# Inverse square roots of head norms in an fp8 attention block: from VectorE instructions to GpSimd instructions

## The chip, the core and the metric

The kernel runs on one NeuronCore of a Trainium2 chip. The metric is the device time of one execution, in microseconds (us); lower is better. Each core has a matrix engine (TensorE, "PE" in the profile, with its weight loads as "PEld"), VectorE ("DVE"), ScalarE ("ACT"), GpSimd ("POOL") and SyncE ("SP"), each with its own instruction queue, worked in order. Engines wait for each other by semaphores.

## What is computed

The program is a decoder of twelve blocks on an activation of 4 batches x 256 tokens x 256 features. The change touches the eleventh block only, an attention with fp8-rounded inputs, of 16 query heads in 4 groups, each head of 128 elements, once on its own tokens and once on a context. Its core, cut from the reference:

```
def _ln(x, w, b):
    mu = jnp.mean(x, axis=-1, keepdims=True)
    var = jnp.mean(jnp.square(x - mu), axis=-1, keepdims=True)
    return (x - mu) * jax.lax.rsqrt(var + EPS) * w + b      # EPS = 1e-05
...
q  = _ln(_fp8_linear_pertensor(ln_out, wq,  wq_scale,  q_in_scale).reshape(b, s, g, hpg, d), qln_w, qln_b)
k  = _ln(_fp8_linear_pertensor(ln_out, wk,  wk_scale,  k_in_scale).reshape(b, s, g, d),      kln_w, kln_b)
v  = _fp8_linear_pertensor(ln_out, wv, wv_scale, v_in_scale).reshape(b, s, g, d)
core = _gqa(q, k, v)
qx = _ln(..., qxln_w, qxln_b);  kx = _ln(..., kxln_w, kxln_b)      # vx likewise, from cond
xout = _gqa(qx, kx, vx)
catq = _div_clamp_fp8(concatenate([core, xout], -1), proj_smooth)
return catq @ wproj.T * (proj_in_scale * proj_w_scale)
```

Every head vector of q, qx, k and kx is thus divided by the square root of its own variance plus 1e-5. The means are already taken out of the weights, so that the variance is the sum of squares over 128.

## The kernel before, in words

The block is `l3_xattn` (line 1558). Its work is cut into 16 passes (`class Pass`, line 1664): pass n handles one of the 4 head groups and one of the 4 batches, so 4 query heads on the own tokens and the same 4 on the context, which makes 8 attention steps i = 0 to 7.

The front of pass n+1 runs during pass n. `product(t, n)` (line 1693) multiplies a tile t of 128 tokens with the weights of q, qx, or k and kx. ScalarE copies the product from PSUM into the tile `x` (128 x 12 heads x 128, line 1706), and squares it into `sq` (line 1708). VectorE sums the squares per head into `ssq` (128 x 12, line 1710). When all three products of a token tile are there, the closure `norm` (line 1712) is due: it turns the 12 sums per token into 12 factors and multiplies `x` by them. In the kernel before, VectorE makes the factors: one multiplication (L1714), `k.rsqrt` (line 108: an addition L113, a shift L117, an affine step on the bits L118, three Newton steps of three instructions each, L120 to L122), and one multiplication (L1716). GpSimd then scales `x` (L1717). Later TensorE transposes the scaled tile (`turned`, L1733).

An attention step is: `scores` (TensorE L1746), maximum (VectorE L344, tile `smx`), exponentials with their sums (ScalarE L354, tile `prob`), `divide` (VectorE's reciprocal L1753 into `sinv`, then GpSimd's multiplication of `prob` by it, L1754), `turn` (TensorE transposes `prob`, L1762, and ScalarE copies it out, L1765), `values` (TensorE L492, VectorE's scaling L1773, and for each second head the rounding to fp8, `bf16_to_e4m3fn`, L205 to L209 on VectorE). `output` (TensorE L1787, VectorE L176) projects the pass before.

The order in which all these go to the engines is written out by hand, and for this block TensorE, ScalarE, VectorE and GpSimd keep it exactly (`ORDERED`, line 2093). In step i the order is: transposes of `x` for the next pass or step (table `TURNS`), scores of i, then `flush` (line 1835: sums of squares and any norm that is due), weight preparation, parts of the next pass's products, `turn` of step i-2, `values` of step i-3, `divide` of step i. By the table `PARTS`, the product of k for token tile 0 is in step 1 and that for tile 1 in step 2, and each is flushed one step later; so the norm of tile 0 is issued in step 2 and that of tile 1 in step 3. The text calls them the first and the second norm of a pass. There are 16 x 2 = 32 norms: two before the first pass, and two in each of the first 15 passes.

In steps that the tables `THIRDS` and `OUT_THIRDS` name, GpSimd also subtracts parts of the weights (L1634, about 1 to 2 us each). In the last two passes, steps of the routing of the next block are put in between.

Of the kernel before, what the change touches and what calls it, by code (L numbers as in the profile page):

```python
# [12 lines left out]
F32 = mybir.dt.float32  # L13
# [7 lines left out]
ALU = mybir.AluOpType  # L21
AX = mybir.AxisListType

P = 128
# [1533 lines left out]
def l3_xattn(k):  # L1558
# [7 lines left out]
    nc, a, v = k.nc, k.a, k.nc.vector  # L1566
# [4 lines left out]
    ws = k.t([P, 12], F32, "ws", 1)  # L1571
# [3 lines left out]
    ws2 = k.t([P, 12], F32, "ws2", 1)  # L1575
    v.tensor_mul(ws2, ws, ws)
    v.tensor_scalar_mul(ws2, ws2, 1.0 / P)
    lnw = k.t([P, 8], F32, "lnw", 1)
    for i, n in enumerate(("q", "qx", "k", "kx")):
        f = 1.0 / math.sqrt(128.0) if i < 2 else 1.0  # L1580
# [83 lines left out]
    class Pass:  # L1664
# [28 lines left out]
        def product(self, t, n):  # L1693

            i = KINDS.index(n)
            if i == 0:
                self.x[t] = k.t([P, 12, P], F32, "x", 3)
                self.ssq[t] = k.t([P, 12], F32, "ssq", 3)
            ps = k.bank()
            if i < 2:  # L1700
                self.thrice(ps, t, n)
            else:
                self.thrice(ps[:, :256], t, "k")
                self.once(ps[:, 256:], t, "kx")
            hs = slice(4 * i, 4 * i + 4)
            nc.scalar.copy(flat(self.x[t][:, hs, :]), ps)
            sq = k.t([P, 4, P], F32, "sq", 2)
            nc.scalar.activation(flat(sq), ps, AF.Square)
            ssq, x = self.ssq[t], self.x[t]
            later.append(lambda: v.tensor_reduce(ssq[:, hs], sq, AX.X, ALU.add))  # L1710

            def norm():
                rs = k.t([P, 12], F32, "hrs", 2)
                v.tensor_tensor(rs, ssq, ws2, ALU.mult)  # L1714
                r = k.rsqrt(rs, 1e-5, "hr")
                v.tensor_tensor(rs, r, ws, ALU.mult)  # L1716
                nc.gpsimd.tensor_tensor(x, x, rs.unsqueeze(2).to_broadcast([P, 12, P]), ALU.mult)  # L1717

            if i == 2:
                later.append(norm)  # L1720
# [135 lines left out]
    for n in range(16):  # L1856
        hg, b = n // 4, n % 4
        nxt = Pass(n + 1) if n + 1 < 16 and b < 3 else None
        for i in range(8):
            g = len(line)  # L1860
# [66 lines left out]
def l3_ffn(k):  # L1927
# [157 lines left out]
BLOCKS = [  # L2085
    l0_attn, l0_xattn, l0_ffn, l1_attn, l1_xattn, l1_ffn,
    l2_attn, l2_xattn, l2_ffn, l3_attn, l3_xattn, l3_ffn,
]

# [136 lines left out]
```

## Time and profile before

| what | value |
|---|---|
| median of 3 runs | 2508.18 us (2507.96 to 2512.40) |
| the profiled execution: its own time | 2510.34 us |
| the profiled execution: its span in the trace | 2508.60 us |
| busy, whole span | PE 1935.5, DVE 1651.4, ACT 1073.0, POOL 731.4 us |
| this block's stretch, 1480 to 2260 us: busy | PE 627.7, DVE 615.1, ACT 451.7, POOL 342.4 of 780 us |
| L1717, scaling of `x` on POOL | 32 times, mean 2754 ns |
| L1754, division of `prob` on POOL | 128 times, mean 1050 ns |
| DMA issues that belong to a norm | none |

The profile is of one execution. A line of its timeline gives the start in us from the beginning of the span, the duration in us, the engine, the source line, the operation, the tiles (out<-in), shapes and a count; a bracket at its end says how long the engine stood idle just before, and what it waited for. A wait for several semaphores is put down to the one that came last by the profile. A line of the list of waits gives the waiting group, what it waited for, the total in us, how often, and the longest. A line of the table by stretches gives the stretch, its length, then busy time of PE, PEld, DVE, ACT and POOL with instruction counts, the granted TensorE clock, the DMA share and GB/s.

### The profile page before, as it was taken

What the parts mean: (1) busy time and instruction counts of PE and PEld (TensorE: products, weight loads), DVE (VectorE), ACT (ScalarE), POOL (GpSimd) and SP (SyncE); (2) the same over time, 40 slices, a digit from 0 to 9 for tenths busy, and PEclk for the clock granted to TensorE, in tenths of its full rate; (3) what the DMA queues carried; (4) which work ended last, traced back from release to release, by engine and by line L of the source; (5) the groups of instructions that cost most, each with busy time, mean ns of one, the idle gap of its engine ahead of it and who ended that gap; (6) DMA issues with size and microseconds to landing.
All of it is one profiled execution on the core that took longest, in us unless ns stands there. A gap on an engine that the chain in (4) does not pass through costs nothing. (4 is left out here: it accounts for less than half of the span.)

```text
span 2508.6 us, 32404 instructions
## 1 busy us (share of the span) xinstructions
PE 1935.5 (77%) x11369; PEld 1322.6 (53%) x11403; DVE 1651.4 (66%) x3987; ACT 1073.0 (43%) x2492; POOL 731.4 (29%) x593
## 2 busy tenths in 40 slices
PE   5999966797885789776577663778988889886784
PEld 3565553454442445543355442556766667764573
DVE  5534448545567543475798896888787777776455
ACT  1322311233345233332666643655656666552242
POOL 1311200001001000010565654335445444433452
PEclk9999987898997899986788876989999999997897
DMA  4001010601502600011012201001010000000796
GB/s 126 1 1 34 1 55 34 208 1 52 168 27 68 191 1 1 13 34 68 9 59 68 85 0 34 1 18 34 1 51 1 16 15 1 2 1 35 256 314 214
DMA packets 100868, 144.10 MB, mean 57 GB/s; under 512 B 10369, under 2 KB 80002, under 8 KB 100450
## 3 DMA queue, kind: packets, MB, share of 16 engines
q1 hardware_dynamic: 91682, 129.35, 16.0%
q0 software_dynamic: 4560, 12.59, 1.3%
q8 instruction: 90, 1.47, 0.2%
q10 hardware_dynamic: 4464, 0.09, 0.1%
q14 instruction: 72, 0.59, 0.1%
HBM read 89.26 MB, written 52.76 MB: 57 GB/s over the span
## 5 line engine op out<-in xcount | busy, mean ns | idle before, releaser
L354 ACT ACTIVATE prob<-mm,smx 128x256 f32<-128x256 f32 x392 | 184.0, 478 | 377.5 <-DVE smx L344 364.6
L548 DVE TENSOR_REDUCE mt<-pair 128x2 f32<-128x512 f32 (+1 forms) x256 | 133.4, 584 | 198.6 <-PE pair L541 198.5
L1350 PE MATMUL acc<-unit,c 128*128 128x256 f32 x512 | 153.4, 448 | 86.3 <-DVE unit L1348 53.6
L1754 POOL TENSOR_TENSOR prob<-prob,sinv 128x512 f32<-128x512 f32 x128 | 134.4, 1050 | 235.8 <-DVE sinv L1753 154.5
L1350 PEld LDWEIGHTS acc<-unit,c 128*128 128x128 f32 x512 | 108.9, 222 | 125.8 <-DVE unit L1348 68.8
L580 ACT ACTIVATE pt<-pair 128x768 f32<-128x768 f32 (+1 forms) x128 | 103.5, 861 | 153.3 <-PE pair L574 153.3
L1346 DVE TENSOR_TENSOR_SCAN h<-da,unit 128x1024 f32<-128x1024 f32 x64 | 146.8, 2293 | 31.4 <-POOL unit L1344 14.5
L1341 ACT ACTIVATE da<-dt,na 128x256 f32<-128x256 f32 x256 | 121.6, 478 | 98.0 <-DVE h L1346 92.5
L1344 POOL TENSOR_TENSOR unit<-du,bcb 128x1024 f32<-128x1024 f32 x64 | 150.0, 2367 | 31.5 <-DVE h L1346 17.7
L344 DVE TENSOR_REDUCE smx<-mm 128x2 f32<-128x512 f32 x196 | 133.2, 680 | 35.5 <-PE mm L480 21.3
L363 POOL TENSOR_TENSOR prob<-prob,sinv 128x512 f32<-128x512 f32 x68 | 71.9, 1058 | 275.9 <-DVE sinv L484 161.7
L492 PE MATMUL acc<-pt,c 128*128 128x256 f32 x512 | 136.3, 390 | 3.8 <-ACT pt L1765 3.8
L1717 POOL TENSOR_TENSOR x<-x,hrs 128x1536 f32<-128x1536 f32 x32 | 88.1, 2754 | 130.3 <-DVE hrs L1716 106.1
L181 POOL TENSOR_TENSOR c<-c,w 128x256 f32<-128x256 f32 x24 | 16.9, 728 | 349.8 <-ACT fqq L268 158.4
L1787 PEld LDWEIGHTS <-cat 128*128 128x128 bf16 x768 | 83.1, 108 | 48.7 <-DVE smx L344 17.3
L1762 PE MATMUL tr<-c,prob 128*128 128x128 f32 x512 | 81.5, 284 | 34.2 <-ACT pt L1765 31.0
L492 PEld LDWEIGHTS acc<-pt,c 128*128 128x128 f32 x512 | 95.0, 197 | 19.1 <-ACT pt L1765 5.4
L1773 DVE TENSOR_SCALAR c<-acc,ism 128x256 bf16<-128x256 f32 x128 | 61.1, 477 | 62.1 <-PE acc L492 62.1
L1733 PE MATMUL tr<-c,x 128*128 128x128 f32 x384 | 59.1, 283 | 47.0 <-ACT pt L1765 36.5
L89 DVE COPY pt<-tr 128x512 f32<-128x512 f32 x66 | 45.6, 691 | 74.7 <-PE tr L367 74.7
L1762 PEld LDWEIGHTS tr<-c,prob 128*128 128x128 f32 x512 | 63.9, 147 | 54.5 <-issue 39.7
L528 PE MATMUL pair<-c,c 128*128 128x256 bf16 x384 | 69.4, 277 | 22.6 <-DVE mt L548 14.3
(558 smaller groups left out, 4987.5 us busy)
## 6 DMA issues: line engine op xcount, KB each, us to landing
xs<-zero SPq DMA_DIRECT2D x3, 12672.0 KB, 43.6
we<-in_L_ffn_w_dram SPq DMA_DIRECT2D x63, 384.0 KB, 4.5
bcb<-bcd SPq DMA_DIRECT2D x32, 512.0 KB, 4.8
xr<-xs SPq DMA_DIRECT2D x8, 528.0 KB, 8.7
w<-in_L_xattn_wproj_dram SPq DMA_DIRECT2D x8, 512.0 KB, 4.1
xr<-ys SPq DMA_DIRECT2D x8, 512.0 KB, 5.0
xr<-xs SPq DMA_DIRECT2D x31, 132.0 KB, 3.5
w<-in_L_xattn_wq_dram SPq DMA_DIRECT2D x5, 512.0 KB, 4.1
```

The source lines that it names most:

```text
L344: nc.vector.tensor_reduce(mx, sc, AX.X, ALU.max, negate=True)
L354: nc.scalar.activation(pr[:, t, :w], sc[:, t, :w], AF.Exp, bias=mx[:, t : t + 1], scale=scale, accum_out=sums[:, t : t + 1],)
L492: k.nc.tensor.matmul(ob[:, :S], v[:, c, :], pt[:, c, :], start=c == 0, stop=c == 1)
L548: nc.vector.tensor_reduce(c, pr[p][:, :, t, :w], AX.X, ALU.max, negate=True)
L580: nc.scalar.activation(o, st[p][:, :, : S + w1], AF.Exp)
L1341: nc.scalar.activation(da[:, i, :], dt[:, c, :], AF.Exp, scale=na[:, col : col + 1])
L1344: nc.gpsimd.tensor_tensor(db, du[:, c : c + 1, :].to_broadcast([P, 4, S]), bb[q], ALU.mult)
L1346: v.tensor_tensor_scan(flat(h), flat(da), flat(db), 0.0, ALU.mult, ALU.add)
L1350: nc.tensor.matmul(ps[:, :S], k.identf, hc[:, i, :], start=q == 0 and i == 0, stop=q == 3 and i == 3)
L1717: nc.gpsimd.tensor_tensor(x, x, rs.unsqueeze(2).to_broadcast([P, 12, P]), ALU.mult)
L1754: nc.gpsimd.tensor_tensor(d["pr"], d["pr"], ri.unsqueeze(2).to_broadcast([P, 2, S]), ALU.mult)
L1762: nc.tensor.transpose(tb[:, c * S + t * P : c * S + (t + 1) * P], pr[:, t, c * P : (c + 1) * P], k.identf)
```

## The change

The factors are made on GpSimd, in eight small instructions ahead of the scaling of `x`, all on 128 x 12 values in float32: the variance plus 1e-5 in two instructions, its power to -0.5 in one (against a 128 x 1 tile of -0.5, read as 128 x 12 by broadcast), one Newton step and the weight scale `ws` in five. A tile for -0.5 is set once by VectorE. The helper `rsqrt` stays as it is and is still used elsewhere. No transfer is added or moved, and the place of `norm` in the order is the same.

```diff
@@ -1575,6 +1575,8 @@
     ws2 = k.t([P, 12], F32, "ws2", 1)
     v.tensor_mul(ws2, ws, ws)
     v.tensor_scalar_mul(ws2, ws2, 1.0 / P)
+    mhalf = k.t([P, 1], F32, "mhalf", 1)
+    v.memset(mhalf, -0.5)
     lnw = k.t([P, 8], F32, "lnw", 1)
...
@@ -1710,11 +1712,17 @@
             later.append(lambda: v.tensor_reduce(ssq[:, hs], sq, AX.X, ALU.add))
 
             def norm():
-                rs = k.t([P, 12], F32, "hrs", 2)
-                v.tensor_tensor(rs, ssq, ws2, ALU.mult)
-                r = k.rsqrt(rs, 1e-5, "hr")
-                v.tensor_tensor(rs, r, ws, ALU.mult)
-                nc.gpsimd.tensor_tensor(x, x, rs.unsqueeze(2).to_broadcast([P, 12, P]), ALU.mult)
+                g = nc.gpsimd
+                e, r, h = (k.t([P, 12], F32, "hr" + n, 2) for n in "erh")
+                g.tensor_tensor(e, ssq, ws2, ALU.mult)
+                g.tensor_scalar_add(e, e, 1e-5)
+                g.tensor_tensor(r, e, mhalf.to_broadcast([P, 12]), ALU.pow)
+                g.tensor_tensor(h, r, r, ALU.mult)
+                g.tensor_tensor(h, h, e, ALU.mult)
+                g.tensor_scalar(h, h, -0.5, 1.5, ALU.mult, ALU.add)
+                g.tensor_tensor(h, h, ws, ALU.mult)
+                g.tensor_tensor(r, r, h, ALU.mult)
+                g.tensor_tensor(x, x, r.unsqueeze(2).to_broadcast([P, 12, P]), ALU.mult)
 
             if i == 2:
                 later.append(norm)
```

## The prediction

> **What bounds the kernel now.** I read the table by stretches, the list of waits over the stretch 1580 to 2200 us, then the timelines of each engine over one pass. First, one stretch and two waits:
>
> ```profile
> 1900.00:2000.00 100.00, 92.21 (x557) 73.77 (x563) 74.70 (x193) 64.92 (x168) 42.91 (x31) 0.98 0.00 1
> ```
> ```profile
> ACT prob L354 <- DVE smx L344: 233.3, 75, 6.6
> POOL x L1717 <- DVE hrs L1716: 88.0, 25, 7.0
> ```
>
> TensorE works 92 of 100 us, so a change here can win only its idle time. Its timeline shows where that lies: in nine of the 15 passes with norms about 2 to 3 us in two pieces, right at the second norm; in four (around 1640, 1828, 2006, 2181 us) a piece of 4.2 to 4.4 us and one of about 1.2; some 44 us in all. ScalarE waits mostly for VectorE's maximum, so VectorE is what makes TensorE late. One pass on VectorE (start, duration):
>
> ```profile
> 2087.41 0.68 DVE L1710 TENSOR_REDUCE ssq<-sq 128x4 f32<-128x512 f32 x1
> 2088.12 0.24 DVE L1714 TENSOR_TENSOR hrs<-ssq,ws 128x12 f32<-128x12 f32 x1
> ...
> 2090.87 0.17 DVE L1716 TENSOR_TENSOR hrs<-hr_y,ws 128x12 f32<-128x12 f32 x1
> 2090.96 0.68 DVE L1710 TENSOR_REDUCE ssq<-sq 128x4 f32<-128x512 f32 x1
> 2091.56 0.47 DVE L1773 TENSOR_SCALAR c<-acc,ism 128x256 bf16<-128x256 f32 x1
> 2092.06 2.02 DVE L205 TENSOR_SCALAR c<-c 128x512 bf16<-128x512 bf16 x1
> 2094.12 0.29 DVE L206 TENSOR_SCALAR c<-c 128x512 int16<-128x512 int16 x1
> ...
> 2096.19 0.67 DVE L344 TENSOR_REDUCE smx<-mm 128x2 f32<-128x512 f32 x1
> 2096.78 1.26 DVE L1710 TENSOR_REDUCE ssq<-sq 128x4 f32<-128x512 f32 x2
> 2098.08 0.17 DVE L1714 TENSOR_TENSOR hrs<-ssq,ws 128x12 f32<-128x12 f32 x1
> ```
>
> The same time on POOL, and the end of it on TensorE:
>
> ```profile
> 2091.19 2.75 POOL L1717 TENSOR_TENSOR x<-x,hrs 128x1536 f32<-128x1536 f32 x1 [2.84 <-DVE hrs L1716]
> 2096.41 1.04 POOL L1754 TENSOR_TENSOR prob<-prob,sinv 128x512 f32<-128x512 f32 x1 [2.48 <-DVE sinv L1753]
> 2101.06 2.75 POOL L1717 TENSOR_TENSOR x<-x,hrs 128x1536 f32<-128x1536 f32 x1 [3.61 <-DVE hrs L1716]
> 2103.77 1.09 POOL L1754 TENSOR_TENSOR prob<-prob,sinv 128x512 f32<-128x512 f32 x1
> ```
> ```profile
> 2104.92 0.42 PEld L1762 LDWEIGHTS tr<-c,prob 128*128 128x128 f32 x4 [0.18 <-POOL prob L1754]
> ```
>
> Two things are to be seen. L205 takes 2.02 us here and 0.29 us where POOL is quiet: it ends just after POOL's L1717 (2091.19 + 2.75 = 2093.94). So what holds VectorE is not only the 14 instructions of the first norm (2088.12 to 2090.96, 2.84 us), but the END of L1717. And the pass runs through both norms in one chain: first sums of squares, factors, L1717, L205 to L209, maximum, sums of squares, factors, L1717, division L1754, and TensorE's transposition at 2104.92.
>
> **The change part by part.** *Removed:* 14 VectorE instructions per norm, 2.84 us, 32 x 2.84 = 91 us. Only the part on the chain above counts.
>
> *Added to POOL:* eight instructions of 12 columns per norm. No row of that size exists; the nearest are small one-input instructions that read each other's results:
>
> ```profile
> 2208.51 0.15 POOL L1398 IOTA in_q<- 128x32 int32 x1
> 2208.73 0.21 POOL L1399 CAST in_q<-in_q 128x32 f32<-128x32 int32 x1
> 2209.01 0.14 POOL L1400 IOTA in_q<- 128x8 int32 x1
> ```
>
> They follow each other at 0.22 and 0.28 us. Two-input rows give the same: L1624 takes 617 ns for 256 columns and 1053 ns for 512, so 181 ns + 1.70 ns a column, 201 ns for 12; with a gap of 0.06 us it is 0.26. I take 0.27 us for each of seven: 1.9 us. The rule that speaks against this is in the Trainium skill, "GPSIMD Engine Reference", section 3.1: an elementwise two-input operation on GpSimd takes 1.96 times VectorE's time. VectorE starts these instructions every 0.206 us, so the rule makes 0.40 each, 0.9 us more per norm. At 12 columns the fixed part decides and the rule was taken at 2048 columns; I go with the rows, and keep +0.9 us for the range.
>
> The eighth is the power, p us from its start to the next start. The trace shows no power on any engine. Lower bound: an ordinary instruction, p = 0.27. Upper bound: a routine that handles the 16 lanes of a GpSimd core one after the other. For a size I use the same page: section 1 gives 16 lanes at 1.2 GHz, section 7 says that a dependent float32 chain costs 4 cycles a step. A logarithm, a product and an exponential by polynomials are perhaps 30 steps; 30 x 4 / 1.2 GHz = 100 ns a column, 12 columns 1.2 us. An estimate, and the number of steps is my guess; unrolled it nears the lower bound, by single lanes it is 16 x 1.2 = 19 us. I take p = 1.2. It lies nearer to the lower bound because every TENSOR_TENSOR row of POOL in this trace (1.7 to 2.3 ns a column) works on all lanes at once.
>
> *The chain with p:* sums end at 2088.09; handover 0.15 (as L1716 to L1717 now); 1.9 + p; L1717 starts at 2090.14 + p and ends at 2092.89 + p; L205 ends 0.14 later as now; L206 to L209 and the reciprocal take 2.11 as now: maximum at 95.14 + p (now 96.19). Maximum and sums 1.86; handover, factors, L1717: 0.15 + 1.9 + p + 2.75; division 1.05: transposition at 2102.9 + 2p, now 2104.92. So each of the nine ordinary passes gains 2.0 - 2p. The break-even is p = 1.0: the power is paid twice in each pass, because the second norm starts behind the first one's L1717. VectorE itself is released by the second norm (maximum of the next step 2 to 3 us earlier), but POOL's division of the same step is queued behind the longer norm, and TensorE's transposition waits for that. This is the wait that takes the place of the one removed.
>
> *The four passes with weight pieces:* L1754 holds POOL until 2169.77, so L1717 comes at 2171.7 + p, now 2172.40; the second norm gives 0.96 - p; sum 1.65 - 2p. The 4.4 us idle there stays, as L205 and L206 still wait for L1717 and for the L1634 behind it.
>
> *Exposed norms:* the two before the first pass (TensorE waits 2.84 and 6.91 us for L1717) and one each in the first and last pass: 3.0 of handover and factors now, 2.05 + p then: 4 x (0.95 - p).
>
> Sum: 9 x (2.0 - 2p) + 4 x (1.65 - 2p) + 4 x (0.95 - p) = 28.4 - 30p us gained. With p = 1.2: 7.6 us lost.
>
> *At nothing:* the memset of -0.5 lies in VectorE's wait of 13.29 us before 1535.70 (otherwise 0.2 us). No DMA is added, and SP's queue is not passed. On POOL, L1634 pieces, the routing's small copies and its indirect DMAs stand behind the norms; POOL is 43% busy, and 2 to 3 us twice a pass leave it under 60%. A one-time loading of code for the power: 0 to 6 us (the same page, section 2.1, for freshly loaded code; no run here shows it); I take 0, since the instruction is of a kind, TENSOR_TENSOR, that has run before.
>
> **The rivals.** *A, the power is cheap (faster).* POOL works through 12 columns unrolled, p = 0.27 to 0.8. Then 28.4 - 30p = 20 to 4 us are gained: 2488 to 2504 us. For it: all POOL rows handle lanes together. It decides up to p = 0.95. *B, the forecast,* p = 0.8 to 1.6, within a few us of 2516. *C, the lock turns over,* p = 1.6 to 3.5. L205 can start at about 2091.4 (TensorE's values end at 2090.89), and L1717 would start at 2090.14 + p: from p = 1.3 on, L205 and then L206, L207 slip in ahead of it. VectorE then is no longer held by the first L1717, and only POOL's own queue counts: 0.15 + 2 x (1.9 + p + 2.75) + 2 x 1.05 from 2088.09 gives a loss of 2p - 5.2 per pass: none before p = 2.6, and at 3.5 some 13 x 1.8 + 4 x 2.5 = 33 us. So 2506 to 2543. *D, single lanes,* p beyond 3.5, to 19: a loss up to 13 x 33 + 4 x 18 = 500 us, POOL becoming the bound of the block, about 3010 us. Against D: every TENSOR_TENSOR row of POOL in this trace works on the lanes together; for it: none of them is more than a product or a difference, so nothing in the trace excludes it.
>
> **How the numbers follow.** The profiled execution took 2510.34 us (span 2508.60 and 1.74 around it); with p = 1.2 it becomes 2517.9. The median of the runs shown is 2.16 lower, 2508.18, so the forecast is 2515.8, say 2516. Chances: A 0.33, B 0.30, C 0.19, D 0.18. Below 2486 I leave 0.05 (TensorE's whole idle time won), above 2600 about 0.13 of D: range 2486 to 2600, which also takes in the 27 us of the rule above. What a measurement can tell from no change is 0.2%, 2503 to 2513 us. Faster: A without its edge, 0.31, and 0.02 of C: 0.33. Same: A's edge, a third of B, a little of C: 0.15. Slower: 0.52.
>
> **What would show it right or wrong.** Right: an instruction of 1.0 to 1.5 us on POOL among seven of 0.2 to 0.3; L205 after the first norm still near 2 us; ScalarE's wait for the maximum well under 233 us; and TensorE's L1762 waiting for POOL's L1754, where that was near nothing. Wrong: a power of 0.3 us (A), or one of many us with L1754 and L1717 behind it (D); L205 at 0.29 us after the first norm (C); small POOL instructions at 0.4 us; or TensorE's pieces of 1.0 us at L1787 gone without a new wait.

## The result, and the profile after

The changed kernel takes 2525.0 us in the median of 4 runs (2524.63 to 2528.04), the kernel before 2509.7 us in the same comparison (2507.96 to 2512.40): a ratio of 1.0061, 95% interval 1.0046 to 1.0077. It is slower. The profiled execution took 2525.25 us, with a span of 2523.5 us, 14.9 us longer than before. The forecast was 2516, within 2486 to 2600.

VectorE did lose its work (busy 1559.6 instead of 1651.4 us) and POOL gained (871.7 instead of 731.4 us). The costliest new groups of POOL, from its groups by form (name, shapes, count, busy us, mean ns of one, idle before):

```profile
L1725 POOL TENSOR_TENSOR x<-x,hrr 128x1536 f32<-128x1536 f32 x32 | 92.5, 2889 | 2.5
L1719 POOL TENSOR_TENSOR hrr<-hre,mhalf 128x12 f32<-128x12 f32 x32 | 73.6, 2300 | 2.7
L1721 POOL TENSOR_TENSOR hrh<-hrh,hre 128x12 f32<-128x12 f32 x32 | 11.5, 360 | 2.5
L1720 POOL TENSOR_TENSOR hrh<-hrr 128x12 f32<-128x12 f32 x32 | 7.0, 217 | 2.5
```

L1719 is the power: 2.30 us. (After the change, `norm` is L1717 to L1725, the division L1762, the transposition of `prob` L1770, that of `x` L1741.) The waits of the stretch 1580 to 2210 us, first after the change, then one of before:

```profile
ACT prob L354 <- DVE smx L344: 194.8, 77, 6.9
PE tr L1770 <- POOL prob L1762: 63.1, 15, 7.8
```
```profile
PE tr L1762 <- POOL prob L1754: 1.0, 1, 1.0
```

ScalarE waits less for VectorE's maximum (194.8, before 233.3 us over 1580 to 2200). TensorE's wait for POOL's division, 1.0 us in all before, is 63.1 us now. It comes 15 times: nine times 3.15 us, and six times 2.46 to 7.83 us, 34.7 us together, in the first pass and the four with weight pieces. The same pass as in the prediction, first on POOL:

```profile
2095.82 0.21 POOL L1717 TENSOR_TENSOR hre<-ssq,ws 128x12 f32<-128x12 f32 x1
2096.11 0.24 POOL L1718 TENSOR_SCALAR hre<-hre 128x12 f32<-128x12 f32 x1
2096.44 2.29 POOL L1719 TENSOR_TENSOR hrr<-hre,mhalf 128x12 f32<-128x12 f32 x1
2098.82 0.21 POOL L1720 TENSOR_TENSOR hrh<-hrr 128x12 f32<-128x12 f32 x1
...
2100.84 3.19 POOL L1725 TENSOR_TENSOR x<-x,hrr 128x1536 f32<-128x1536 f32 x1
2103.99 1.04 POOL L1762 TENSOR_TENSOR prob<-prob,sinv 128x512 f32<-128x512 f32 x1
2104.99 0.21 POOL L1717 TENSOR_TENSOR hre<-ssq,ws 128x12 f32<-128x12 f32 x1
...
2109.44 2.79 POOL L1725 TENSOR_TENSOR x<-x,hrr 128x1536 f32<-128x1536 f32 x1
2112.19 1.09 POOL L1762 TENSOR_TENSOR prob<-prob,sinv 128x512 f32<-128x512 f32 x1
```

POOL is never idle for more than about 0.1 us from 2095.82 to 2113.28. VectorE and TensorE in the same time:

```profile
2099.01 0.29 DVE L205 TENSOR_SCALAR c<-c 128x512 bf16<-128x512 bf16 x1
...
2101.41 0.67 DVE L344 TENSOR_REDUCE smx<-mm 128x2 f32<-128x512 f32 x1
...
2109.66 2.72 DVE L207 TENSOR_SCALAR c<-c 128x512 bf16<-128x512 bf16 x1
```
```profile
2109.15 1.03 PE L1754 MATMUL mm<-xTk,xTqx 128*128 128x256 f32 x4
2113.33 1.12 PE L1770 MATMUL tr<-c,prob 128*128 128x128 f32 x4 [3.15 <-POOL prob L1762]
2114.24 1.92 PE L492 MATMUL acc<-pt,c 128*128 128x256 f32 x4
```

(By the lock the text means what the prediction read from the trace before: VectorE's L205, begun beside POOL's scaling, ended only with it.) After the first norm L205 now takes 0.29 us: during the long power nothing holds VectorE, and L205 to L209 slip in ahead of most of the scaling. After the second norm L207 is still held, for 2.72 us. TensorE runs through both places where it stood before:

```profile
2097.96 1.47 PE L1787 MATMUL mm<-wps,cat 128*128 128x256 bf16 x12 [1.01 <-ACT prob L354]
2103.62 0.66 PE L1733 MATMUL tr<-c,x 128*128 128x128 f32 x4 [1.14 <-ACT pt L1765]
```

Now it waits 3.15 us in one piece instead, for the division of step 3. In all nine ordinary passes this wait is 3.15 us to the hundredth.

Its next matmuls are slow: four of L492 take 1.92 us, 1.03 elsewhere. The table by stretches (after the five busy times: granted TensorE clock, DMA share, GB/s) gives, just behind that wait in the changed kernel, and behind the later of two waits in the kernel before:

```profile
2113.30:2117.00 3.70, 3.67 (x13) 3.21 (x14) 2.43 (x6) 1.50 (x5) 1.14 (x2) 0.50 0.00 0
```
```profile
2103.60:2107.60 4.00, 3.98 (x25) 3.41 (x26) 3.86 (x8) 1.72 (x4) 1.85 (x3) 1.00 0.00 0
```

The clock is halved. Behind the nine waits of 3.15 us it was 0.50 to 0.64 for about 4 us in seven cases, and 1.00 in two. Before, the idle time of these passes came as 1.0 and then 1.1 to 2.0 us, and the clock behind them stayed at 1.00, except once: behind the 2.02 us at 2058.63 it was 0.57.

The length of passes, from one step-0 maximum (L344) to the next, read off the timelines (us; passes 3 and 4 are ordinary, pass 5 has weight pieces at its norms, pass 6 in its later steps):

| kernel | pass 3 | pass 4 | pass 5 | pass 6 | median | ratio to before, 95% interval |
|---|---|---|---|---|---|---|
| before | 39.4 | 39.0 | 51.9 | 46.2 | | |
| changed | 40.2 | 41.3 | 52.3 | 45.1 | 2525.0 | 1.0061 (1.0046 to 1.0077) |
| changed, again | 40.2 | 41.3 | 52.3 | 45.0 | 2524.1 | 1.0047 (1.0029 to 1.0066) |
| no power | 38.3 | 37.8 | 48.1 | 43.6 | 2485.1 | 0.9893 (0.9860 to 0.9926) |
| no Newton step | 39.8 | 39.5 | 49.1 | 45.3 | 2504.1 | 0.9967 (0.9958 to 0.9976) |
| both norms behind the division | 41.3 | 40.9 | 50.1 | 47.2 | 2523.0 | 1.0039 (1.0028 to 1.0050) |
| power twice | 46.6 | 45.3 | 54.5 | 46.2 | 2584.7 | 1.0290 (1.0256 to 1.0324) |
| second norm behind step 4 | 41.5 | 41.4 | 47.0 | 44.4 | 2508.4 | 0.9998 (0.9989 to 1.0006) |
| before, scaling behind | 41.2 | 40.8 | 52.5 | 45.4 | 2530.5 | 1.0073 (1.0049 to 1.0097) |
| no factors | 38.6 | 36.8 | 45.9 | 41.8 | 2452.2 | 0.9757 (0.9728 to 0.9786) |
| wait filled | 40.2 | 39.9 | 51.6 | 44.8 | 2518.1 | 1.0037 (1.0029 to 1.0045) |
| second norm behind step 3 | 36.9 | 36.5 | 46.3 | 44.4 | 2470.6 | 0.9835 (0.9815 to 0.9855) |
| the same, no Newton step | 40.8 | 39.2 | 45.0 | 45.8 | 2486.0 | 0.9895 (0.9877 to 0.9914) |

The kernel before had a median of 2508 to 2513 us in these comparisons, so ratios are compared, not medians. In pass 3 the changed kernel loses 0.8 us (a wait of 3.15 for 1.01 and 1.13, clock kept), in pass 4 it loses 2.3 (a wait of 3.15 for 1.00 and 1.08, and a slow clock).

Counted over fourteen passes, from the first scaling of `x` in one to that in the next, the profiled execution loses 15.4 us: 15.9 in the nine ordinary passes, and in sum nothing (0.5 gained) in the other five. There TensorE's long wait has moved as well, for instance before and after:

```profile
2006.35 2.72 PE L1787 MATMUL mm<-wps,cat 128*128 128x256 bf16 x12 [4.37 <-ACT prob L354]
```
```profile
2020.87 1.12 PE L1770 MATMUL tr<-c,prob 128*128 128x128 f32 x4 [6.88 <-POOL prob L1762]
```

The clock behind both is 0.50.

### The profile page after: what moved, and what is told of

Its sections match the earlier page's. It is cut to its first block, busy times and chain, and to the rows that moved or that the text cites. A ratio compares the mean times of both kernels' runs of the same rounds, so it can differ in the third digit from the quotient of the medians.

```text
span 2523.5 us, 32246 instructions
## 1 busy us (share of the span) xinstructions
PE 1946.0 (77%) x11403; PEld 1334.3 (53%) x11403; DVE 1559.6 (62%) x3540; ACT 1073.8 (43%) x2492; POOL 871.7 (35%) x849
## 3 DMA queue, kind: packets, MB, share of 16 engines
q1 hardware_dynamic: 91682, 129.35, 15.9%
## 5 line engine op out<-in xcount | busy, mean ns | idle before, releaser
L1762 POOL TENSOR_TENSOR prob<-prob,sinv 128x512 f32<-128x512 f32 x128 | 134.7, 1054 | 195.5 <-DVE sinv L1761 132.7
L344 DVE TENSOR_REDUCE smx<-mm 128x2 f32<-128x512 f32 x196 | 133.8, 682 | 59.3 <-PE mm L1754 30.5
L1770 PE MATMUL tr<-c,prob 128*128 128x128 f32 x512 | 84.6, 291 | 89.2 <-POOL prob L1762 65.4
L492 PE MATMUL acc<-pt,c 128*128 128x256 f32 x512 | 146.2, 412 | 3.7 <-ACT pt L1773 3.7
L1770 PEld LDWEIGHTS tr<-c,prob 128*128 128x128 f32 x512 | 64.1, 149 | 111.9 <-POOL prob L1762 72.4
L492 PEld LDWEIGHTS acc<-pt,c 128*128 128x128 f32 x512 | 100.4, 208 | 19.9 <-ACT pt L1773 5.4
L1773 ACT COPY pt<-tr 128x512 f32<-128x512 f32 x128 | 77.4, 604 | 42.1 <-PE tr L1770 42.1
L1725 POOL TENSOR_TENSOR x<-x,hrr 128x1536 f32<-128x1536 f32 x32 | 92.5, 2889 | 2.5
L2077 POOL DMA_INDIRECT ys<-yr,to x63 | 61.1, 971 | 77.0 <-DVE yr L2076 46.3
```

Of the source, the lines that this page charges most:

```text
L344: nc.vector.tensor_reduce(mx, sc, AX.X, ALU.max, negate=True)
L492: k.nc.tensor.matmul(ob[:, :S], v[:, c, :], pt[:, c, :], start=c == 0, stop=c == 1)
L1725: g.tensor_tensor(x, x, r.unsqueeze(2).to_broadcast([P, 12, P]), ALU.mult)
L1762: nc.gpsimd.tensor_tensor(d["pr"], d["pr"], ri.unsqueeze(2).to_broadcast([P, 2, S]), ALU.mult)
L1770: nc.tensor.transpose(tb[:, c * S + t * P : c * S + (t + 1) * P], pr[:, t, c * P : (c + 1) * P], k.identf)
```

## The experiments

My theory after the result: the power makes POOL's chain of two norms and two divisions longer than the rest of the pass; TensorE waits at its end. The rivals were the number of small POOL instructions and the lock between POOL and VectorE, the place in POOL's queue alone, and the slow clock.

**The power by itself.**

```diff
...
+    for width in (1, 4, 12, 48, 192):
+        for op in (ALU.mult, ALU.pow):
+            nc.gpsimd.tensor_tensor(pout[:, :width], pin[:, :width], pm.to_broadcast([P, width]), op)
```

> The changed kernel with ten more POOL instructions at the start of the third block, where POOL has nothing else: a multiplication and a power of 1, 4, 12, 48 and 192 columns each. Theory (POOL works all lanes of a column together, and a power costs a fixed number of cycles a column): the power takes 2.3 us at 12 columns and a straight line, about 0.17 us a column: 0.4, 0.9, 2.3, 8.5 and 34 us; multiplications 0.2 to 0.6 us. Rival (a large fixed part, such as code that is fetched for each power): near 2 us at 1 column and little growth.

Groups of one multiplication and one power each:

```profile
L728 POOL TENSOR_TENSOR pout<-pin,pm 128x1 f32<-128x1 f32 x2 | 0.8, 391 | 31.5 <-DVE pm L724 31.4
L728 POOL TENSOR_TENSOR pout<-pin,pm 128x4 f32<-128x4 f32 x2 | 1.2, 614 | 0.2
L728 POOL TENSOR_TENSOR pout<-pin,pm 128x12 f32<-128x12 f32 x2 | 2.5, 1248 | 0.2
L728 POOL TENSOR_TENSOR pout<-pin,pm 128x48 f32<-128x48 f32 x2 | 8.3, 4134 | 0.2
L728 POOL TENSOR_TENSOR pout<-pin,pm 128x192 f32<-128x192 f32 x2 | 31.5, 15772 | 0.2
```

The mean of 128x12 is 1248 ns and the power there 2.29 us, so the multiplication is 0.2. The power of 192 columns took 30.99 us. So the power is a straight line: (30.99 - 2.29) / 180 = 0.159 us a column, and 2.29 - 12 x 0.159 = 0.38 us at zero columns. There is no fixed cost of microseconds. Nor does a first-time cost stand out: the first power of the program, of one column, and a multiplication together took 0.78 us, where the line and 0.2 us make 0.74. The kernel ran once, but these durations come from its trace.

**The power taken away, and doubled.**

```diff
-    v.memset(mhalf, -0.5)
+    v.memset(mhalf, 2.0**-14)
...
-                g.tensor_tensor(r, e, mhalf.to_broadcast([P, 12]), ALU.pow)
+                g.tensor_tensor(r, e, mhalf.to_broadcast([P, 12]), ALU.mult)
```

> The power is replaced by a multiplication by a small constant in the same place, so the factors are no inverse roots; everything else of the change stays. Theory (the power's 2.3 us is paid twice in each pass, on POOL's queue): POOL's eight small instructions at 0.3 us each make the norm shorter than the 3.1 us of before, about 1 us a pass is gained, 2494 us (2488 to 2502). Rival (the number of small POOL instructions, and their taking turns with VectorE at the shared memory port, cost the time, whatever the power takes): still 2515 or more.

0.9893: about 27 us faster than before, a larger gain than the expected range allowed, and the rival is out: eight small instructions on POOL are no loss as such. With so short a norm L205 stands behind the first scaling again (1.98 us at 1690.34).

```diff
                 g.tensor_tensor(r, e, mhalf.to_broadcast([P, 12]), ALU.pow)
+                g.tensor_tensor(r, e, mhalf.to_broadcast([P, 12]), ALU.pow)
```

> The power is computed twice into the same tile, all else as in the changed kernel. Theory: 2.38 us more per norm, 4.8 us per pass, all on POOL's chain: 2525 + 13 x 4.8 + 4 x 2.4 = 2597 us (2585 to 2610). Rival (the power lies beside other work, the loss is elsewhere): under 2545.

2584.7, a little under the range of 2585 to 2610; the ordinary wait of TensorE is 3.74 us longer than with one power, not 4.8:

```profile
1768.95 1.11 PE L1771 MATMUL tr<-c,prob 128*128 128x128 f32 x4 [6.89 <-POOL prob L1763]
```

The power is on the path; each further us of it costs about 3.74 / 4.76 = 0.8 of what I reckoned. Where the other fifth goes is open.

**Four instructions less.**

```diff
-                g.tensor_tensor(h, r, r, ALU.mult)
-                g.tensor_tensor(h, h, e, ALU.mult)
-                g.tensor_scalar(h, h, -0.5, 1.5, ALU.mult, ALU.add)
-                g.tensor_tensor(h, h, ws, ALU.mult)
-                g.tensor_tensor(r, r, h, ALU.mult)
+                g.tensor_tensor(r, r, ws, ALU.mult)
```

> The Newton step is left out (four instructions of POOL fewer per norm, the power stays), so the factors are a little less exact. Theory (POOL's chain of two norms and two divisions sets the pass): 4 x 0.3 us less per norm, 2.4 us per pass, so TensorE's wait of 3.15 us per pass falls under 1 us: 2500 us (2494 to 2510). Rival (the slow matmuls after the wait, or the port, are the cost): no more than 8 us below the changed kernel, 2517 or more.

0.9967, as the theory said; it beats the kernel before by 0.3%. But I had reckoned with a wait under 1 us in the ordinary passes, and that did not come. TensorE there:

```profile
1950.47 1.47 PE L1791 MATMUL mm<-wps,cat 128*128 128x256 bf16 x12 [1.15 <-ACT prob L354]
1957.72 0.66 PE L1766 MATMUL tr<-c,prob 128*128 128x128 f32 x4 [1.43 <-POOL prob L1758]
```

The wait is 2.58 us instead of 3.15, in two pieces, and the clock keeps up. The first piece is the one of before: with a shorter norm, POOL's scaling again catches VectorE's rounding (L206 takes 2.73 us at 1944.14).

**The place in POOL's queue.** First, both norms behind the division of their step:

```diff
-                later.append(norm)
+                later.append(lambda: behind.append(norm))
...
             now.divide(i)
+            for f in behind:
+                f()
+            behind.clear()
```

> The changed kernel with all POOL instructions of a norm moved behind the division of the same step. Theory (TensorE waits for the division of step 3, which is queued behind the second norm): the division of step 3 then stands behind the first norm only, TensorE waits about 1.4 us instead of 3.15 per pass, 2500 us (2490 to 2512). Rival (POOL's added work costs as such, by the port or by its sum): about 2525 as now.

2523: a miss. The wait only moved:

```profile
2110.89 1.09 PE L1742 MATMUL tr<-c,x 128*128 128x128 f32 x8 [1.44 <-POOL x L1726]
2120.57 0.66 PE L1771 MATMUL tr<-c,prob 128*128 128x128 f32 x4 [2.50 <-POOL prob L1763]
```

1.44 us for the first norm's `x` and 2.50 for the division of step 4. Two norms of 8 us side by side, with the divisions at them, fill POOL for 19 us (2102.64 to 2121.51); being behind one division is not enough. So I pulled them apart:

```diff
-                later.append(norm)
+                later.append(norm if t == 0 else lambda: behind.append(norm))
...
             now.divide(i)
+            while i == 4 and behind:
+                behind.pop(0)()
```

> The changed kernel with only the second norm of a pass moved on POOL, from step 3 to behind the division of step 4; the first stays. Theory (two norms of 8 us within two steps are more than POOL can do there, so some division is late wherever they stand together): apart, no division waits more than a few tenths, TensorE's 3.15 us per pass goes, and the change keeps what it takes from VectorE: 2488 us (2478 to 2500). Rival (POOL's added work costs by the shared port or as a sum, wherever it stands): 2515 or more.

0.9998: 12 to 16 us better than the changed kernel (ratios 1.0047 and 1.0061), but not the 2488 of the theory. It was one step too late: TensorE's transposition of `x` now waits for the second norm, and its clock falls to 0.57 behind it, while POOL had stood idle for 5.59 us ahead of the division of step 4:

```profile
1753.52 1.64 PE L1742 MATMUL tr<-c,x 128*128 128x128 f32 x8 [3.17 <-POOL x L1726]
```

With `i == 3` instead of `i == 4`:

> The changed kernel, the first norm in its place, the second behind the division of step 3 on POOL (in between its own place and that of the run that put it behind step 4's). Theory (POOL stands idle some 5.6 us there, so the norm fits between two divisions and is done before its transposition): neither the division of step 3 nor the transposition of x waits long; at most 1 to 2 us a pass of wait for the division of step 4: 0.990 to 0.998 of the kernel before. Rival (POOL's sum binds the pass in any order): 1.000 or more.

2470.6 us, 0.9835 of the kernel before: more than was expected, and the fastest that computes the whole. VectorE in an ordinary pass, first and second norm:

```profile
1891.29 0.30 DVE L205 TENSOR_SCALAR c<-c 128x512 bf16<-128x512 bf16 x1
...
1901.28 0.34 DVE L205 TENSOR_SCALAR c<-c 128x512 bf16<-128x512 bf16 x1
1901.65 0.29 DVE L206 TENSOR_SCALAR c<-c 128x512 int16<-128x512 int16 x1
1901.98 0.29 DVE L207 TENSOR_SCALAR c<-c 128x512 bf16<-128x512 bf16 x1
```

Neither rounding is caught, and in passes 4, 8, 11 and 12, of 36.5 to 36.6 us, TensorE has no wait of 0.9 us or more at the norms. With the Newton step left out as well:

> The same place for the second norm, and without the Newton step (four POOL instructions less per norm). Theory: POOL's norm takes 6.8 instead of 8 us, so the rest of the waits goes: 0.985 to 0.994 of the kernel before, below the version without the Newton step alone (0.9967). Rival (once POOL's norm is that short, the place does not matter, or VectorE's rounding is caught by the second scaling instead): within 0.002 of 0.9967.

0.9895: in the expected range and faster than the version without the Newton step alone, but slower than with the step, because what the rival named has happened. POOL's scaling and VectorE's rounding, first norm:

```profile
1901.47 2.76 POOL L1722 TENSOR_TENSOR x<-x,hrr 128x1536 f32<-128x1536 f32 x1
```
```profile
1901.32 0.29 DVE L205 TENSOR_SCALAR c<-c 128x512 bf16<-128x512 bf16 x1
1901.65 2.72 DVE L206 TENSOR_SCALAR c<-c 128x512 int16<-128x512 int16 x1
```

Less work on POOL brings its scaling into the rounding: it starts 3.29 us after the norm's first instruction, with the step 4.96 us. L206 waits out all of it. At the second norm of the pass L207 does:

```profile
1913.22 2.73 DVE L207 TENSOR_SCALAR c<-c 128x512 bf16<-128x512 bf16 x1
```

**The kernel before with its scaling behind the division** (the same edit as for both norms, but only L1717 is moved):

> The kernel before (factors on VectorE) with only POOL's scaling of x moved behind the division of the same step. Theory (the end of POOL's scaling holds VectorE's rounding, and the division of step 3 stands behind it): both go, TensorE loses most of its 2 to 3 us per pass: 2485 us (2475 to 2498). Rival (VectorE's own 2.84 us of factors is what makes it late): 2505 or more.

1.0073: slower, against the theory; the rival allowed the number, but its reason does not explain a loss. POOL's first scaling, and VectorE's first factor instruction of the second norm:

```profile
1924.61 2.75 POOL L1718 TENSOR_TENSOR x<-x,hrs 128x1536 f32<-128x1536 f32 x1
```
```profile
1925.27 2.12 DVE L1715 TENSOR_TENSOR hrs<-ssq,ws 128x12 f32<-128x12 f32 x1
...
1931.93 2.64 DVE L205 TENSOR_SCALAR c<-c 128x512 bf16<-128x512 bf16 x1
```

The first scaling (POOL, 1924.61 to 1927.36) now holds up the second norm's factors, and the second one the rounding. This is the counterpart of the version with both norms behind (1.0039), not of the best one: the kernel before with only its second scaling moved was not run. So it is not shown how much of 0.9835 needs the factors on POOL, and how much the place alone would give.

**No factors at all.** POOL scales by `ssq`; this leaves the inverse roots out.

> The factors are left out: POOL scales x by the sums of squares themselves, so neither VectorE nor POOL makes an inverse root. It bounds what any cheaper way to make them can win. Theory (TensorE's idle time at the norms, some 44 us, is all there is): 2470 us (2460 to 2482). Rival (the scaling itself, with the port, is what holds the pass): 2490 or more.

2452.2, lower than either side said; passes 4, 8, 11 and 12 take 36.5 to 36.9 us, passes 3 and 7 take 38.6. That the best version takes 36.5 to 36.6 us in the former too says that there the factors cost nothing any more; over the whole it is still 0.8% behind.

**The slow clock.**

```diff
-            ps = k.bank()
+            ps = self.out = k.bank()
...
+            if i == 5 and last:
+                for _ in range(16):
+                    nc.tensor.matmul(last.out[:, D:], k.identb, last.cats[0][:, 0, :], start=True, stop=True)
             if g >= 2:
```

> The changed kernel with 16 idle matmuls of 256 columns (some 1.8 us) ahead of the transposition of step 3's probabilities, where TensorE waits 3.15 us; their result is not used. Theory A (after an unbroken wait of 3.15 us TensorE's granted clock falls to 0.5 to 0.6 for some 4 us in most passes, and that is about 8 to 10 us of the loss): the clock stays at 1.0, 2517 us (2511 to 2521). Theory B (the waits alone make the loss, the clock adds nothing): 2524 or more, up to 2540 where the filling doesn't fit the wait.

2518.1, as theory A said. The wait is 1.41 us plus the filling, so the transposition comes no sooner:

```profile
2104.69 0.66 PE L1770 MATMUL tr<-c,prob 128*128 128x128 f32 x4 [1.41 <-POOL prob L1762]
```

But behind it:

```profile
2104.70:2108.70 4.00, 4.00 (x29) 3.52 (x30) 2.97 (x7) 2.04 (x6) 1.65 (x2) 1.00 0.00 0
```

The clock stays at 1.00 behind all nine of these waits, and pass 4 takes 39.9 instead of 41.3 us. How much of the loss this is in the whole is less sure: the ratios 1.0061 and 1.0047 of the changed kernel against 1.0037 make 2.5 to 6 us, not the 8 to 10 of theory A, and the intervals of the latter two overlap.

> The changed kernel as it is, on the chip of these runs, to compare the others with: 0.5 to 0.8% over the kernel before.

1.0047: the loss is there again, a little under the range expected.

## Why the prediction came out as it did

- *The time.* 2525 lies in the range and on the side that was forecast; the loss is 15 us where 8 were forecast. That it came so near is luck: the power was dearer than taken, and the path was another, on which it costs less. The two errors partly cancel.
- *The power.* The term that was mis-sized is p: 1.2 us was taken, 2.38 us from start to start was measured. It is not the lower bound and not the single lanes (19 us): 0.159 us a column, where my guess of 30 dependent steps made 0.100.
- *The small instructions.* 0.27 us was taken for each of seven; the quiet second norm has 0.28 to 0.32. The rows of the small POOL instructions were right, and the 0.40 us that the rule set against them would have made is not seen at 12 columns.
- *The chain.* The forecast's way (L205 still behind the first L1717, the power paid twice through VectorE) is wrong: with p = 2.38 its sum would be 28.4 - 30 x 2.38, a loss of 43 us. What happened is rival C, to which 0.19 was given: VectorE's rounding slips ahead and POOL's queue counts. It gave 2506 to 2543 us for p = 1.6 to 3.5, and 2525 lies in it, but that does not confirm its sum.
- *C's own sum* at p = 2.38 is 2 x 2.38 - 5.2 = -0.44, no loss, and pass 3 lost 0.8 us. The rest may be the small instructions (14 x 0.03 = 0.4 us) and two of the first norm, L1724 at 0.65 and L1725 at 3.19 us (0.44 us each over 0.21 and 2.75), begun while VectorE's L208 and L209 ran: -0.44 + 0.4 + 0.88 = 0.84. This sum was made afterwards, and no run tests it. C left out the clock too.
- *The passes with weight pieces.* The forecast let their 4.4 us stay; at p = 2.38 it has 4 x (1.65 - 4.76), 12 us lost. Their waits moved to POOL's division and grew to 5.7 to 7.8 us, yet counted from first scaling to first scaling these four gained 2.3 us in sum; why is open.
- *The new wait* was named: TensorE's L1762 (now L1770) for POOL's division, 63.1 us in all. That ScalarE's wait for the maximum falls was right as well (233.3 to 194.8).
- *Not foreseen:* what a wait in one piece does to the clock. The idle time in an ordinary pass grew by only about 1 us, but as one piece of 3.15 us.
- *Rival A* fell by its price, not by its mechanism: without the power's time the kernel gains 27 us (20 forecast), with L205 behind the first scaling as A had it.

## What to carry to other kernels

A special function on GpSimd is to be measured by the column before it is moved there: here 12 values per partition took 2.3 us, where VectorE needed 2.84 us for all 14 of its instructions. When work goes to an engine that has a queue of other work and holds up VectorE, and is held up by it, its place in that queue can matter as much as its length: the same instructions gave 1.006, 1.004, 1.000 and 0.984 of the time before, and at the best place a version with fewer of them was slower again (0.990). Look at what the end of the long instruction now meets, and whether the idle time of TensorE comes in one piece.

## What was not expected of the hardware

- TensorE's granted clock fell to 0.50 to 0.64 for about 4 us behind seven of nine waits of 3.15 us, and did not behind waits of 1.41 us (nine of nine). Over this block (1580 to 2205 us) in all fourteen traces, it was under 0.9 in the next 4 us behind none of 153 waits of 1.2 to 1.8 us, 56 of 126 of 1.8 to 2.8 us, 51 of 74 of 2.8 to 3.8 us, and behind all 74 longer ones. The Trainium skill, "TensorE: Matmul & The Clock Gate", Part 1, has the clock halved after an idle window of about 3.4 us; here less was enough, and not every time.
- POOL's power runs at 0.159 us a column of 128 values with 0.38 us on top, a multiplication of 12 columns at 0.2 us.
- VectorE's two-input instruction of 12 columns took 2.12 us (0.17 alone) beside POOL's scaling, and ended with it (at 1925.27 + 2.12 = 1927.39, the scaling at 1927.36); the lock is not only for one-input instructions like L205. It works the other way too: POOL's L1725 took 3.19 us the nine times that it began beside VectorE's L209, and 2.75 to 2.79 the other 23 times.
